# Residual sums of a graph-network stack: accumulating transfers in place of GpSimd sums, and a re-drawn order

## The chip, the cores and the metric

The kernel runs on one core of a Trainium2 chip. A core has five engines that run side by side, each through its own list of instructions in order: PE (TensorE, matrix products), DVE (VectorE), ACT (ScalarE), POOL (GpSimd) and SP (SyncE, which here only issues transfers). They wait for each other by semaphores. Transfers (DMA) run on 16 engines of their own. The metric is the time of one execution on the device in microseconds; the median of several runs counts, and less is better.

## What is computed

128 graphs of 64 nodes with 256 features go through four layers, each a residual step: normalise, rectify, apply a graph network, add to the input.

```python
# layers 0 and 1: attention over the neighbours
h = jnp.maximum(_layernorm(x, axis=-1), 0.0)
x = x + _L0_gnn_ref(h, adj, ...)     # 4 heads, ends in elu(...)
h = jnp.maximum(_layernorm(x, axis=-1), 0.0)
x = x + _L1_gnn_ref(h, adj, ...)     # 1 head, ends in elu(...)
# layer 2: products gated by a relation, summed over neighbours, relu
h = jnp.maximum(_layernorm(x, axis=-1), 0.0)
x = x + _L2_gnn_ref(h, nodemask, adj, ...)
# layer 3: three steps of a gated recurrence
h = jnp.maximum(_layernorm(x, axis=-1), 0.0)
x = x + _L3_gnn_ref(h, adj, ...)
# inside layer 3, three times:
#   m = h @ weight[i];  aggr = A^T m;  h = gru_cell(aggr, h)
```

Everything is float32. The change concerns the additions `x + ...` of layers 0, 1 and 3.

## The kernel before

**Tiling.** The 8192 rows of x are cut into 16 groups of 512 rows (8 graphs). A group's x lies in SBUF as the tile `xg`, 128 partitions by 4 by 256. For each group the layers 0, 1 and 2 run once (`first_layer`, `second_layer`, `third_layer`), then `before` normalises for layer 3, and a `Recurrence` object runs its three steps. Two groups' recurrences are interleaved with the first three layers of later groups, so that PE always has something of another group to do. Groups 0 and 1 are cut finer and take other ways through the early layers (`AHEAD = 2`); "from the third group on" means `g >= AHEAD`.

**Layers 0 and 1** are `attention(g, ...)`: statistics of `xg` on DVE (`st`, `mv`), `rstd` and `nm` on POOL, normalised values on ACT (`hn`), a transposition by DVE and through DRAM (`way`), products `mm` on PE, the attention factors `t` on DVE, and the weighted sums on PE into `o`. It ends in `elu_add` (line 850): with e = exp(min(o, 0)), the tile `em` becomes max(e - 1, o), and `engine.tensor_tensor(src, src, em, ALU.add)` adds it to `xg`. In the profile `em` is called hn, since it takes one of the three shared buffers of that name; the sum is the row xg<-xg,hn. The next layer's statistics read `xg` after it.

**Layer 3.** A step works out gates by products of 128x128 blocks with 256 columns (tiles `sy` and `sz`), each result picked up by DVE or ACT and put together in `hT`, `r` and `z`, partly by DVE instructions with two SBUF operands (`hT<-r,hT`, `r<-z,r`), partly by POOL (`r<-hT,hT`, and `aS`, `hS`, sums of the next step's operands). After the last step the state is brought back through DRAM (`back_by_dma`, into `hnat`), `finish` (line 1054) adds it to `xg` on POOL (row xg<-xg,hnat), and SP stores the result. The very last group instead turns its result on PE and adds on DVE.

**The order.** The program does not emit as it goes. A recording layer (`Plan`) notes every operation with an estimated cost, `forward` lists them engine by engine by due time, `backward` works out new due times, and `emit` (line 504) repeats this `PASSES` times from a random `SEED`, keeps the best, then shifts the due times of whole jobs by the pseudo-random moves named in `MOVES`, and emits the outcome once. All operations so recorded carry line 550 in the profile (blocks of 64x64 products line 842). So new numbers in `SEED` and `MOVES` mean another order on all engines. A transfer is planned with an issue time of `ISSUE` = 665 ns on its engine and a landing worked out from `cost` (line 584). Where the planner leaves PE idle in the first 115 us, `emit` puts warm-up products (line 1664) whose results nobody reads.

Of the kernel before, what the change touches and what calls it, by code (L numbers as in the profile page):

```python
# [13 lines left out]
ALU = mybir.AluOpType  # L14
# [3 lines left out]
S = 32  # L18
# [3 lines left out]
K = D // P  # L22
# [200 lines left out]
class Plan:  # L223
# [30 lines left out]
    def note(self, engine, call, cost, writes, reads, after=(), port=0.0, dma=False):  # L254
# [23 lines left out]
            b.ops.append(op)  # L278
        return op

    PASSES, SEED, SPREAD = 40, 35, 50.0
    MOVES = (
        10, 23, 28, 30, 40, 45, 69, 85, 99, 108, 114, 116, 126, 132, 141, 159, 210, 227, 236, 241, 319, 326, 339, 343,
        354, 365, 383, 426, 448, 489, 544, 596, 636, 646, 651, 652, 704, 736, 741, 742, 743, 752, 760, 807, 869, 944,
        951, 987, 991, 1089, 1101, 1110, 1124, 1248, 1251, 1273, 1452, 1492, 1498, 1501, 1678, 1834, 1893, 1966, 2005,
        2010, 2196, 2270, 2336, 2377, 2433, 2441, 2584, 2658, 2695, 2697, 2873, 3006, 3016, 3031, 3058, 3081, 3167,
        3224, 3271, 3376, 3444, 3459, 3524, 3571, 3664, 3704, 3719, 3750, 3772, 3786, 3953, 4165, 4169, 4192, 4344,
        4481, 4581, 4610, 4913, 4970, 5115, 5123, 5266, 5287, 5433, 5732, 6133, 6139, 6156, 6871, 6933, 7088, 7813,
        7842, 8883, 9045, 9231, 9268, 10172, 10189, 10284, 10634, 10814, 10991, 13029, 13068, 13352, 13896, 14140,
        16577, 16772, 17027, 533, 1980, 2724, 3643, 4767, 7708,  # L290
    )
    LEEWAY = {"PE": 100.0, "DVE": 100.0, "Activation": 100.0, "Pool": 100.0, "SP": 300.0, "-": 0.0}
    OVERLAP = {"DVE": 83.0, "Activation": 95.0, "Pool": 43.0}
# [35 lines left out]
    def forward(self):  # L329

        for b in self.bases:
            b.left, b.end, b.spot = len(b.ops), 0.0, None
        pools = {id(b.pool): b.pool for b in self.bases}.values()
        for pool in pools:
            pool.clear()
        for op in self.ops:
            op.job.left, op.waits = op.job.size, len(op.after)
        free = dict.fromkeys([*ENGINES.values(), "-"], 0.0)
        ready = {e: [] for e in free}
        held = {"DVE": 0.0, "Pool": 0.0}  # L340
        wire, parts = 2500.0, False
        order, self.replaced = [], []

        def enter(op):
            t = 0.0
            for other, data in op.after.items():
                late = other.end + self.LATENCY
                if other.engine == op.engine and not (other.dma and data):
                    late = other.start if op.engine in ("PE", "SP") or not data else other.end + 35.0
                if late > t:  # L350
                    t = late
            op.ready = t
            ready[op.engine].append(op)

        def spots(op, t):

            places = []
            for b in op.needs:
                if b.spot is None:
                    taken = [tag for x, tag in places if x.pool is b.pool]  # L360
                    tag = b.pool.place(b, taken)
                    if tag is None:
                        return None, t
                    places.append((b, tag))
                    t = max(t, b.pool.released(tag, b, taken.count(tag)))
            return places, t

        for op in self.ops:
            if not op.waits:
                enter(op)  # L370
        while len(order) < len(self.ops):
            best = None
            for e, ops in ready.items():
                leeway, first, found = self.LEEWAY[e], 1e18, []
                for op in ops:
                    t = op.ready if op.ready > free[e] else free[e]
                    if t > first + leeway or best is not None and t > best[0] + leeway:
                        continue
                    if any(j.left for j in op.job.after):
                        continue  # L380
                    places, t = spots(op, t)
                    if places is not None:
                        first = min(first, t)
                        found.append((t, op, places))
                found = [(t, op.due, op, places) for t, op, places in found if t <= first + leeway]
                if found:
                    found = min(found, key=lambda f: (f[1], f[0]))
                    if best is None or found[:2] < best[:2]:
                        best = found
            assert best is not None, "nothing can be emitted"  # L390
            t, _, op, op.places = best
            e = op.engine
            ready[e].remove(op)
            for b, tag in op.places:
                old = b.pool.put(b, tag)
                if old is not None:
                    self.replaced.append((old, op))
            if e == "-":
                for pool in pools:
                    pool.open = True  # L400
            op.start, op.idle = t, t - free[e]
            if op.dma:
                free[e] = t + self.ISSUE
                wire = max(wire, t + 1350.0) + op.cost
                op.end = wire + 400.0
            else:
                took = op.cost
                if e == "PE":
                    took -= self.TURN if op.parts and parts else 0.0
                    parts = op.parts  # L410
                elif op.port:
                    other = "Pool" if e == "DVE" else "DVE"
                    took = max(took, held[other] + min(op.port, took) - t)
                    held[e] = t + took
                op.end = t + took + (165.0 if e == "PE" else 0.0)
                free[e] = t + took - op.overlap
            for b in op.bases:
                b.left -= 1
                b.end = max(b.end, op.end)
            op.job.left -= 1  # L420
            order.append(op)
            for other in op.then:
                other.waits -= 1
                if not other.waits:
                    enter(other)
        return max(free.values()), order

    def backward(self, end):
# [12 lines left out]
        for op in self.ops:  # L441
            op.took = min(op.end - op.start, 4500.0) if op.dma else op.end - op.start
            op.held = (op.took if op.engine in ("DVE", "Pool") else op.cost) - op.overlap
            if op.dma:
                op.held = self.ISSUE
            op.rank = op.end + self.random.gauss(0.0, self.SPREAD)

        def limit(op, late):
# [135 lines left out]
def cost(engine, method, args, kwargs):  # L584

    n = elements(args[0])
    if engine == "tensor":
        m = elements(args[2] if method == "matmul" else args[0])
        return (m / 1.2 + 2.5) * (1 if method == "transpose" else 2)
    if engine == "sync" or method == "dma_start":  # L590
        to, of = args[:2]
        tag = to.base.tag if isinstance(to, View) else None
        rate = {"way": 450.0, "fine": 220.0, "t0": 190.0, "t1": 190.0}.get(tag, 150.0 if tag in (None, "at", "eg", "o", "row0", "row1") else 290.0)
        if isinstance(of, View) and of.base.tag in ("way", "fine"):
            rate = 170.0 if of.base.tag == "way" else 125.0
        return n * to.shape[0] * 4 / rate
    if engine == "vector":
        if method == "bn_stats":
            return 400.0
        if method == "tensor_reduce":  # L600
            n = elements(args[1])
        plain = method == "tensor_scalar" and not any(isinstance(a, View) for a in args[2:4])
        return 150.0 + n * (0.53 if plain and n >= 512 else 1.04)
    if engine == "scalar":
        return 150.0 + 0.86 * n if method in ("copy", "mul") else 310.0 + 0.73 * n
    if ALU.pow in args:
        return 1000.0
    return 200.0 + 2.1 * n if method != "memset" else 100.0 + 0.85 * n
# [3 lines left out]
def kernel(  # L612
# [237 lines left out]
    def elu_add(work, src, o, engine, by_scalar=False):  # L850
# [6 lines left out]
            nc.vector.tensor_scalar(em, o, 0.0, None, op0=ALU.min)  # L857
            nc.scalar.activation(em, em, AF.Exp)
        nc.vector.scalar_tensor_tensor(em, em, -1.0, o, op0=ALU.add, op1=ALU.max)
        engine.tensor_tensor(src, src, em, ALU.add)  # L860

    def block_diagonal(dst, src, scalar, op):

# [116 lines left out]
    class Recurrence:  # L980
# [72 lines left out]

        def finish(self):

            to = self.src.rearrange("p n (k i b) -> p (n k) i b", k=K, b=S)
            nc.gpsimd.tensor_tensor(to, to, spread(self.hnat), ALU.add)
            self.store(self.src, slice(None))

        def step(self, i, back=True, in_parts=False):  # L1060
# [159 lines left out]
    with ExitStack() as s1:  # L1220
# [175 lines left out]
        def attention(g, p0, n, layer, heads, we, pool):  # L1396
# [59 lines left out]
                edges = mt[:, q : q + m, None, :].to_broadcast([P, m, heads, N])  # L1456
                nc.vector.tensor_tensor(t4, t4, edges, ALU.min)
            o = aggregate_graphs(pool, psum, t, wv, heads, g < 16)
            elu_add(pool, src, o, nc.vector if g < 1 else nc.gpsimd, g >= AHEAD)

        def first_weights():
            e0 = once.tile([P, K, 2 * H], F32, name="e0")
# [419 lines left out]
```

## Time and profile before

| | us |
|---|---|
| runs | 1311.43, 1312.52, 1318.44; median 1312.52 |
| the profiled execution | 1311.0 |
| its span, first to last instruction | 1309.2 |
| first product of the recurrence starts at | 95.3 |
| last product of 256 columns starts at, on PE | about 1298 |

Busy shares of the span are 98% for PE, 80% for DVE, 66% for ACT and 53% for POOL; the granted PE clock is 0.997 of full speed. A row of the profile gives engine, operation, destination tile, source tiles, shapes, how often, the total and mean time, and the idle time of the engine just before such instructions with what ended it. "L550" is the line of the recording layer and says nothing about the place; one goes by the tiles. A product of 32-bit numbers appears as two MATMUL records, and the end of a record is modelled: starts are what one can trust.

The chain of work that ended last runs through PE for 86% of the span, through DVE for 6%, through POOL and ACT for 3% each. The views that the prediction is worked out from are shown there.

### The profile page before, as it was taken

To read this page: it belongs to the slowest core of one execution; us is meant where nothing else is said; L and a number is where in the kernel's file an instruction comes from. 1 tells how busy PE (TensorE), PEld (TensorE's weight loads), DVE (VectorE), ACT (ScalarE), POOL (GpSimd) and SP (SyncE) were. 2 spreads that over 40 slices of the span, in tenths; PEclk is the share of its full clock that TensorE was granted. 3 is DMA by queue.
4 is the path that set the end of the run, shared out by engine and by line. 5 is a ranking of instruction groups with operands and counts; after the bars stand their busy time and mean duration, and the time that the engine had idled before them with its cause. 6 is when DMAs were issued, how large, how long until landed. Compare 5 with 4: busy or idle time off the path is not lost.

```text
span 1309.2 us, 27708 instructions
## 1 busy us (share of the span) xinstructions
PE 1288.8 (98%) x9761; PEld 1024.4 (78%) x9761; DVE 1052.5 (80%) x2532; ACT 857.7 (66%) x2179; POOL 700.3 (53%) x859
## 2 busy tenths in 40 slices
PE   9999999999999999999999999999999999999996
PEld 8667877788777887777787787778878787778885
DVE  7887788968879798887968879796969877776665
ACT  7876666766667676666657657766766667655543
POOL 4845454645555473655527456373747556435443
PEclk9999999999999999999999999999999999999998
DMA  8202133343343434334333444433334433322112
GB/s 249 87 19 63 33 118 106 112 128 118 118 125 111 141 98 135 131 104 122 128 112 114 121 136 122 130 130 102 118 98 138 146 86 117 104 77 71 60 65 69
DMA packets 139349, 142.64 MB, mean 109 GB/s; under 512 B 46912, under 2 KB 126272, under 8 KB 139200
## 3 DMA queue, kind: packets, MB, share of 16 engines
q1 hardware_dynamic: 137856, 140.50, 35.1%
q8 instruction: 80, 1.31, 0.4%
q14 instruction: 69, 0.57, 0.1%
q10 hardware_dynamic: 1344, 0.27, 0.1%
HBM read 78.39 MB, written 61.80 MB: 107 GB/s over the span
## 4 chain that ended last, share of the span: by engine, by line
PE 86%; DVE 6%; POOL 3%; ACT 3%; issue 1%; DMA 1%; SPq 0%; DVEq 0%; ACTq 0%; POOLq 0%
PE sy L550 35%; PE sz L550 26%; PE mm L550 16%; PE mm L842 3%; PE tp L842 3%; DVE hT L550 2%; DVE t L550 1%; PE tp L550 1%; POOL rstd L550 1%; ACT hn L550 1%; PE sz L1664 1%; PE tq L842 1%; POOL xg L550 1%; DVE r L550 1%; DMA t<-row 1%
## 5 line engine op out<-in xcount | busy, mean ns | idle before, releaser
L550 POOL TENSOR_TENSOR r<-hT,hT 128x256 f32<-128x256 f32 x192 | 154.4, 811 | 237.7 <-ACT hT L550 236.9
L550 DVE SCALAR_TENSOR_TENSOR hT<-r,hT 128x256 f32<-128x256 f32 (+1 forms) x290 | 186.4, 647 | 27.1 <-ACT r L550 24.7
L550 PE MATMUL sy<-aS,wsum 128*128 128x256 f32 x576 | 172.8, 384 | 1.9 <-DVE hT L550 1.9
L550 PE MATMUL sy<-hS,wsum 128*128 128x256 f32 x576 | 171.2, 383 | 2.0 <-ACT z L550 1.5
L550 PE MATMUL sz<-hS,whh 128*128 128x256 f32 x576 | 171.4, 383 | 0.6 <-DVE z L550 0.5
L550 PE MATMUL sz<-aS,wc 128*128 128x256 f32 x576 | 164.9, 382 | 0.9 <-DVE hT L550 0.9
L550 DVE TENSOR_TENSOR hT<-hT,sz 128x256 f32<-128x256 f32 x288 | 117.7, 410 | 42.6 <-PE sz L550 38.9
L550 ACT ACTIVATE hT<-hT,bi 128x256 f32<-128x256 f32 x192 | 95.8, 504 | 51.8 <-DVE hT L550 51.3
L550 PEld LDWEIGHTS sy<-hS,wsum 128*128 128x128 f32 x576 | 107.1, 190 | 27.8 <-issue 5.9
L550 POOL TENSOR_TENSOR rstd<-var,mhalf 128x4 f32<-128x4 f32 (+1 forms) x70 | 76.7, 1095 | 97.2 <-ACT var L550 92.5
L550 PEld LDWEIGHTS sy<-aS,wsum 128*128 128x128 f32 x576 | 107.2, 190 | 25.1 <-issue 6.0
L550 PEld LDWEIGHTS sz<-aS,wc 128*128 128x128 f32 x576 | 108.2, 190 | 21.6 <-issue 5.8
L550 PEld LDWEIGHTS sz<-hS,whh 128*128 128x128 f32 x576 | 107.5, 190 | 21.9 <-issue 5.9
L550 ACT ACTIVATE hT<-sy,bh 128x256 f32<-128x256 f32 x192 | 90.0, 469 | 49.8 <-PE sy L550 48.6
L550 POOL TENSOR_TENSOR aS<-aT 128x256 f32<-128x256 f32 x96 | 79.0, 823 | 81.6 <-ACT aT L550 78.8
L550 PE MATMUL mm<-wl,hT 128*128 128x512 f32 x248 | 118.9, 595 | 1.3 <-DVE u L550 1.0
L550 ACT ACTIVATE hn<-xg,nm,rstd 128x256 f32<-128x256 f32 x200 | 109.4, 594 | 15.1 <-POOL nm L550 11.9
L550 ACT COPY z<-sy 128x256 f32<-128x256 f32 x192 | 70.2, 369 | 66.8 <-PE sy L550 65.2
L550 DVE TENSOR_TENSOR hT<-hT,sy 128x256 f32<-128x256 f32 x192 | 79.2, 412 | 37.5 <-PE sy L550 35.1
L550 DVE TENSOR_TENSOR z<-sz,z 128x256 f32<-128x256 f32 x192 | 79.6, 416 | 25.7 <-PE sz L550 23.4
L550 DVE BATCH_NORM_STATS2 st<-xg 128x6 f32<-128x256 f32 x256 | 95.6, 406 | 5.1 <-DMA xg<-in_x_dram 3.1
L550 POOL TENSOR_TENSOR hS<-hT 128x256 f32<-128x256 f32 x96 | 81.8, 852 | 24.5 <-DVE hT L550 15.2
(212 smaller groups left out, 3197.9 us busy)
## 6 DMA issues: line engine op xcount, KB each, us to landing
way<-tb SPq DMA_DIRECT2D x59, 512.0 KB, 2.7
hnat<-way SPq DMA_DIRECT2D x184, 128.0 KB, 3.0
way<-hn SPq DMA_DIRECT2D x42, 512.0 KB, 3.0
hn<-way SPq DMA_DIRECT2D x168, 128.0 KB, 2.9
xg<-in_x_dram SPq DMA_DIRECT2D x15, 512.0 KB, 4.3
out_dram<-xg SPq DMA_DIRECT2D x15, 512.0 KB, 3.0
t<-row SPq DMA_DIRECT2D x28, 256.0 KB, 4.0
hT<-way SPq DMA_DIRECT2D x52, 128.0 KB, 2.9
```

The source lines that it names most:

```text
L550: return do(*[real(a) for a in args], **{k: real(v) for k, v in kwargs.items()})
L842: nc.nc.tensor.matmul(*[real(x) for x in product], start=True, stop=True)
L1664: nc.spare = lambda: psum.spare and nc.nc.tensor.matmul(pause, warm, warm, start=True, stop=True)
```

## The change

Three things change.

- `elu_add` gets no engine (`None`) in layers 0 and 1 from the third group on. Then it issues a transfer from POOL's queue that reads `em` and adds it to `xg` in place (`accum_op`), 512 KB, 28 times in all. The planner gets a cost for it (line 591 on: bytes / 200 per ns, so 2.6 us on the wire), and an issue time of 1000 ns on POOL.
- `finish` adds in two pieces of two row blocks each; the store still follows both.
- `SEED` and `MOVES` are new, so the order of all instructions is.

```diff
-    PASSES, SEED, SPREAD = 40, 35, 50.0
+    PASSES, SEED, SPREAD = 40, 47, 50.0
     MOVES = (
-        10, 23, 28, 30, 40, 45, 69, 85, 99, 108, 114, 116, 126, 132, 141, 159, 210, 227, 236, 241, 319, 326, 339, 343,
...
+        27, 28, 39, 43, 47, 48, 58, 65, 69, 92, 99, 136, 172, 201, 203, 236, 247, 266, 267, 280, 285, 286, 311, 315,
...
     )
...
             if op.dma:
-                free[e] = t + self.ISSUE
+                free[e] = t + (1000.0 if e == "Pool" else self.ISSUE)
                 wire = max(wire, t + 1350.0) + op.cost
...
             if op.dma:
-                op.held = self.ISSUE
+                op.held = 1000.0 if op.engine == "Pool" else self.ISSUE
...
     if engine == "sync" or method == "dma_start":
         to, of = args[:2]
+        if "accum_op" in kwargs:
+            return n * to.shape[0] * 4 / 200.0
...
         nc.vector.scalar_tensor_tensor(em, em, -1.0, o, op0=ALU.add, op1=ALU.max)
-        engine.tensor_tensor(src, src, em, ALU.add)
+        if engine is None:
+            nc.gpsimd.dma_start(src, em, accum_op=ALU.add)
+        else:
+            engine.tensor_tensor(src, src, em, ALU.add)
...
         def finish(self):
 
-            to = self.src.rearrange("p n (k i b) -> p (n k) i b", k=K, b=S)
-            nc.gpsimd.tensor_tensor(to, to, spread(self.hnat), ALU.add)
+            m = G // 2
+            for p in range(0, G, m):
+                to = self.src[:, p : p + m].rearrange("p n (k i b) -> p (n k) i b", k=K, b=S)
+                nc.gpsimd.tensor_tensor(to, to, spread(self.hnat[:, :, p : p + m]), ALU.add)
             self.store(self.src, slice(None))
...
-            elu_add(pool, src, o, nc.vector if g < 1 else nc.gpsimd, g >= AHEAD)
+            elu_add(pool, src, o, nc.vector if g < 1 else nc.gpsimd if g < AHEAD else None, g >= AHEAD)
```

In the built programs the counts of instructions differ only where the diff says so, and in the warm-up products: 48 before, 61 after. Before any recurrence product starts, both programs put the same kinds and nearly the same numbers of other products on PE.

## The prediction

> **What bounds the kernel now.** First the busy table and the busy time by stage. Columns of the second view: stage, its length, then busy us of PE, weight loads, DVE, ACT, POOL, granted clock, DMA share, GB/s.
>
> ```profile
> PE 1288.8 (98%) x9761; PEld 1024.4 (78%) x9761; DVE 1052.5 (80%) x2532; ACT 857.7 (66%) x2179; POOL 700.3 (53%) x859
> ...
> 95.00:1280.00 1185.00, 1177.65 (x8977) 943.07 (x8970) 961.82 (x2262) 773.35 (x1920) 639.26 (x757) 1.00 0.36 109
> 1280.00:1310.00 30.00, 18.79 (x84) 14.76 (x82) 16.67 (x35) 8.72 (x20) 8.74 (x9) 0.85 0.24 74
> ```
>
> PE is the bound, and in the long middle stage (95 to 1280 us) it is idle for only 7.4 us of 1185. But a matmul's recorded time ends later than its successor starts, so short gaps are inside "busy". I therefore read starts in the timeline: a product with 256 columns is two records and takes 0.43 us from start to start when nothing delays it (385.39 to 385.83 around the first stall below). Measured against such undisturbed pitches, PE loses in the middle stage: 11 stalls of at least 0.165 us, 9.1 us together; 140 gaps of about 0.105 us, 14.7 us together; and 116 similar gaps (11.0 us) in front of blocks of 64x64 tiles, which come with the blocks. So an order of work can win back at most 9.1 + 14.7 = 23.8 us here, 1.8% of the time.
>
> Next, who makes the long stalls. The groups of POOL and DVE that bear on it (busy us, mean ns; idle before):
>
> ```profile
> L550 POOL TENSOR_TENSOR xg<-xg,hn 128x1024 f32<-128x1024 f32 x28 | 69.4, 2478 | 22.8 <-DVE hn L550 22.8
> L550 POOL TENSOR_TENSOR xg<-xg,hnat 128x1024 f32<-128x1024 f32 x15 | 36.5, 2436 | 20.3 <-DMA hnat<-way 20.2
> ...
> L550 DVE SCALAR_TENSOR_TENSOR hT<-r,hT 128x512 f32<-128x512 f32 x94 | 82.2, 879 | 0.9
> ```
>
> and the timeline of POOL, DVE and PE at three stalls (start, length):
>
> ```profile
> 383.75 2.80 POOL L550 TENSOR_TENSOR xg<-xg,hn 128x1024 f32<-128x1024 f32 x1
> ...
> 384.60 2.50 DVE L550 SCALAR_TENSOR_TENSOR hT<-r,hT 128x512 f32<-128x512 f32 x1
> ...
> 385.83 0.59 PE L550 MATMUL sz<-hS,whh 128*128 128x256 f32 x2
> 387.90 0.70 PE L550 MATMUL sy<-hS,wsum 128*128 128x256 f32 x2 [1.48 <-ACT z L550]
> ```
>
> ```profile
> 524.16 2.43 POOL L550 TENSOR_TENSOR xg<-xg,hnat 128x1024 f32<-128x1024 f32 x1 [2.33 <-DMA hnat<-way]
> ...
> 524.29 2.91 DVE L550 SCALAR_TENSOR_TENSOR hT<-r,hT 128x256 f32<-128x256 f32 x2
> ...
> 525.94 0.59 PE L550 MATMUL sy<-aT,wsum 128*128 128x256 f32 x2
> 528.19 0.70 PE L550 MATMUL sy<-aS,wsum 128*128 128x256 f32 x2 [1.66 <-DVE hT L550]
> ```
>
> ```profile
> 1290.30 2.35 POOL L550 TENSOR_TENSOR xg<-xg,hnat 128x1024 f32<-128x1024 f32 x1 [6.65 <-DMA hnat<-way]
> ...
> 1291.10 1.83 DVE L550 SCALAR_TENSOR_TENSOR hT<-r,hT 128x256 f32<-128x256 f32 x1
> ...
> 1293.32 0.48 PE L550 MATMUL sz<-aS,wc 128*128 128x256 f32 x1 [0.87 <-DVE hT L550]
> ```
>
> In each, a DVE instruction with two SBUF operands starts inside POOL's long sum and does not end until POOL's has: 2.50 us where the same form takes about 0.7 us. The gate chain of the recurrence stands still behind it, and PE runs out of operands. Note 0.70 instead of 0.59 at the restart: after each wait another 0.11 us goes, which is what the 140 short gaps are.
>
> **What the Trainium skill says.** "SBUF — State Buffer", section "Who interferes with whom": a VectorE instruction with two SBUF inputs contends with a GpSimd instruction that reads SBUF, and the later one blocks fully. The lines above agree (2.50 us, ended by POOL's end at 386.55). The same page, section "SBUF: two separate sides": a transfer issued from GpSimd needs GpSimd to write descriptors, which VectorE in a two-port mode holds up; the trace of before has no such transfer. "DMA: Bandwidth & Descriptors", section "Rules for kernel authors": an accumulating transfer reads its destination and writes it later, so readers must wait for its semaphore; here that is the next layer's statistics. Price, same page, "Anatomy of one DMA": 2.0 us + bytes / 436 GB/s, so 3.2 us for 512 KB as an estimate, and about 1 us to the first byte (section "Specifications"). SP's transfers of that size land in 3.0 and 4.3 us:
>
> ```profile
> way<-hn SPq DMA_DIRECT2D x42, 512.0 KB, 3.0
> ...
> xg<-in_x_dram SPq DMA_DIRECT2D x15, 512.0 KB, 4.3
> ```
>
> **The change, part by part.** Against the span of 1309.2 us:
>
> 1. *28 sums leave POOL.* 69.4 us of POOL work go; 28 issues come. What each issue costs POOL is not in the trace: between 0 and the old 2.48 us, and I take 1 us. Queued behind it on POOL in the new order are the recurrence's own operations (r, hS or aS in nearly all cases), so they wait less than before. The gain is in the lock. Over the trace, DVE instructions with two SBUF operands run 82.6 us longer than their undisturbed length; 15.9 us of it (16 collisions) lie under xg<-xg,hn. PE's stalls that follow from these sums: 1.64 (386.0), 1.17 (639.0, where DVE's transpose waited for the sum's end) and 0.41 us (1027, the buffer of the summand free too late) = 3.2 us. All gone: -3.2.
>
> 2. *The 15 last sums in halves.* Each half should take some 1.2 us (the rows with 512 columns have a mean of 1315 ns). In the new POOL order the halves mostly stand next to each other (11 of 15 with nothing between), so a DVE instruction that comes during the first may get in between them or not. Stalls from these sums: 1.82 (526.2), 0.91 (219.8), 1.03 (1292.1) = 3.8 us; bounds 0 and -3.8; I take half: -1.9. Of their 8.9 us of DVE lock time half would go, 4.4.
>
> 3. *Short gaps.* DVE's lock loss falls by (15.9 + 4.4) / 82.6 = 25%. If the short gaps fell alike: 14.7 x 0.25 = 3.6; but many come from ACT or from the order, so I take half: -1.8.
>
> 4. *Another order.* All engines' orders are re-dealt. Of the 23.8 us some 16 are left after 1 to 3. Before's own remaining stalls (1.38 at 600.0, where the mask product waited for t<-row; 0.68 at 1140, POOL's rstd) are accidents of an order; a new one has its own. I see one thing in the new order that leaves room: between a sum's summand and the next statistics, DVE has 9 instructions (median), 4.4 us of work by the starts of such rows, where there were 6 to 7 with 2.8 us. Bounds: -12 and +6. I take -4.
>
> 5. *The start.* The program puts warm-up products where its planner left PE idle before 115 us: 61 instead of 48. At 0.22 us each that is 2.9 us more planned idleness ahead of the first recurrence step (the other products ahead of it, each at its pitch, are the same: 74.5 against 75.6 us). Bounds 0 and +2.9; part of it will sit in gaps that PE had anyway. I take +2.
>
> 6. *The wait for the landing.* Today the statistics follow the sum's end by some 0.5 us (median of the 28). Then: 1 us of issue and about 4 us to land (between the 3.0 and 4.3 above, and it reads two operands), 5 us from the summand. The new order's 4.4 us of DVE work take 4.4 / 0.81 = 5.4 us at DVE's 81% load of the middle stage. So the landing is just hidden where the order has its median; in five of the 28 places DVE has under 2.7 us of work there, and there DVE waits some 2 us, as it waited before for POOL. What stalled DVE by about 1 us 16 times cost PE 3.2 us, so 5 x 2 us cost some 2, less what other idle time covers. Bounds 0 and +17 (rival C). I take +1. The summand's buffer (three of them, shared) is held some 2.5 us longer too; the same cover.
>
> Turns into and out of 64x64 blocks stay: 128 blocks against 130. The DMA engines get 28 x 0.5 MB more to write at a share of 0.36: nothing.
>
> Sum: -3.2 - 1.9 - 1.8 - 4 + 2 + 1 = -7.9, so a span of 1301.3 us. The profiled execution took 1311.0 us, 1.8 more than its span; the median of the runs is 1312.5, another 1.5 above. Forecast for the median: 1312.5 - 7.9 = 1304.6 us, -0.6%. A measurement here tells no change from up to about 0.5%, 6.6 us, so the forecast lies barely outside.
>
> **The rivals.**
>
> *B, a draw.* The lock stalls go, but the new order earns nothing and the start costs in full: -3.2 - 1.9 - 1.8 + 2.9 + 1.5 = -2.5, 1310.0 us. For it: 11 long stalls in 1185 us is already few. Against it: the short gaps are half of what can be won, and DVE is freed of a quarter of its lock time.
>
> *C, slower: the landing at the head of DVE's queue.* The statistics stand in DVE's queue; if the landing is late, everything behind them (gates of the recurrence) stands. If issue to landing takes 7.5 us, because accumulation runs at half rate or descriptors wait, DVE stalls 2 us at 28 places, 56 us; at the 0.3 that PE lost per us of DVE's long blocks (3.2 of 15.9 us, plus its short gaps) that is +17: -2.5 - 1.5 + 17 = +13, 1325.5 us. It decides from about 6.5 us on, where the cost passes the 4 us saved plus the 6.6. Against it: 3.0 to 4.3 us for like transfers, and DMA engines idle two thirds of the time.
>
> *D, the order bears much more:* items 1 and 2 in full (-7.0), short gaps and remaining stalls halved (-10), +2: 1297.5 us.
>
> **How the numbers follow.** Forecast 0.50 (own range 1299 to 1309: 0.42 of it faster, 0.08 within 0.5%); B 0.30 (0.03, 0.26, 0.01 slower); C 0.12 (0.02 within, 0.10 slower); D 0.08, faster. Together: faster 0.53, within 0.5% 0.36, slower 0.11. The range 1297 to 1316 leaves out C and half of D.
>
> **What would show it.** Items 1 and 2: no DVE instruction of 2 us or more beside POOL; mean of the 128x512 form of hT<-r,hT down from 879 towards 800 ns. 3 and 4: starts of products 0.43 us apart with fewer breaks; idle PE in 95 to 1280 below 4 us. 5: the first product of sy later than its 95.3 us. 6: waits of DVE's st for the transfer into xg in sum below 10 us, landing near 4 us. Wrong would be: such waits above 30 us, landing above 6 us, or a first recurrence step 5 us later.

## The result, and the profile after

The kernel after takes 1326.43 us (median of 6 runs, 1324.90 to 1330.28), the one before 1312.68 us (6 runs, 1311.43 to 1318.44): a ratio of 1.0107, 95% interval 1.0090 to 1.0125. It is slower by 14 us, where the forecast was 1304.6 us and the range ended at 1316. The profiled execution took 1330.28 us with a span of 1328.5; it is the longest of the six, 3.9 us over their median, so single sums from it are read with that in mind.

The busy table and the busy time by stage of the kernel after (columns as before: stage, length, busy us of PE, weight loads, DVE, ACT, POOL, clock, DMA share, GB/s):

```profile
PE 1303.0 (98%) x9787; PEld 1028.0 (77%) x9787; DVE 1041.2 (78%) x2532; ACT 856.9 (65%) x2179; POOL 650.3 (49%) x874
...
95.00:1280.00 1185.00, 1170.59 (x8815) 925.86 (x8814) 940.15 (x2237) 764.55 (x1904) 581.23 (x760) 1.00 0.42 120
```

POOL is busy for 50 us less than before and DVE for 11 us less, as intended. Yet PE's idle time in the middle stage doubled, from 7.4 to 14.4 us. Measured from start to start against undisturbed pitches, as in the prediction, PE lost there:

| 95 to 1280 us | before | after |
|---|---|---|
| stalls of at least 0.165 us | 11, 9.1 us | 43, 22.3 us |
| gaps of about 0.105 us | 140, 14.7 us | 172, 18.2 us |
| gaps in front of 64x64 blocks | 116, 11.0 us | 108, 10.2 us |

The first product of the recurrence starts at 99.2 us instead of 95.3. So the 19.3 us between the two spans are 13.2 of long stalls, 3.5 of short gaps and 3.9 of a later start, less about 1.3 in turns and at the end. Seven of the 43 stalls are no waits: they are records of four products that ran at half clock, shown below.

Now the parts that the change touched. First POOL's and DVE's groups (busy us, mean ns of one; idle before):

```profile
L549 POOL TENSOR_TENSOR xg<-xg,hnat 128x512 f32<-128x512 f32 x30 | 39.6, 1334 | 19.4 <-DMA hnat<-way 18.3 <-issue 1.1
L549 POOL DMA_DIRECT2D xg<-hn x28 | 25.7, 920 | 8.5 <-DVE hn L549 8.5
```

```profile
L550 DVE SCALAR_TENSOR_TENSOR r<-z,r 128x512 f32<-128x512 f32 x94 | 78.9, 845 | 12.0 <-POOL r L550 5.9 <-ACT z L550 5.8 <-ACT hT L550 0.2
...
L549 DVE SCALAR_TENSOR_TENSOR r<-z,r 128x512 f32<-128x512 f32 x94 | 82.0, 878 | 15.1 <-POOL r L549 9.8 <-ACT z L549 4.9
L549 DVE SCALAR_TENSOR_TENSOR hT<-r,hT 128x512 f32<-128x512 f32 x94 | 75.3, 807 | 0.9
```

(The first of the last three lines is from before.) An issue holds POOL for 0.92 us. The form of hT<-r,hT with 512 columns fell from 879 to 807 ns, as it was to do, but r<-z,r did not: 845 before, 878 now. Then the transfers (queue; packets, MB and share; and the median from issue to landing) and DVE's waits for them (us in total, times, longest):

```profile
q0 software_dynamic: 4032, 14.68, 5.8%
...
xg<-hn POOLq DMA_DIRECT2D x28, 512.0 KB, 4.6
```

```profile
DVE st L549 <- DMA xg<-hn: 5.7, 5, 1.9
...
DVE hn L549 <- DMA xg<-hn: 2.9, 1, 2.9
```

A transfer lands 4.6 us after its issue, and DVE's statistics (st) wait for one at five places only, 5.7 us in all. By the prediction's own marks the landing was fine. Two other marks failed: PE's idle time was to be below 4 us and is 14.4, and no DVE instruction was to take 2 us or more beside POOL, where gates of 2.3 to 3.2 us now stand within 4 us of an issue at four places. The last line is another wait: DVE's transpose into hn does not read the sum, it wants the *buffer* of the summand, which the transfer holds until it lands. It makes the longest stall of PE. The timeline of POOL, DVE and PE there:

```profile
409.66 0.91 POOL L549 DMA_DIRECT2D xg<-hn  x1
410.60 0.74 POOL L549 TENSOR_TENSOR aS<-aT 128x256 f32<-128x256 f32 x1
```

```profile
410.75 0.62 DVE L549 TENSOR_SCALAR top<-amax 128x4 f32<-128x4 f32 x1
414.26 1.25 DVE L549 STREAM_TRANSPOSE hn<-hn 128x1024 f32<-128x1024 f32 x1 [2.90 <-DMA xg<-hn]
415.44 1.25 DVE L549 TENSOR_TENSOR u<-mm,bl 128x512 f32<-128x512 f32 x2
```

```profile
414.08 0.59 PE L549 MATMUL sz<-aT,wc 128*128 128x256 f32 x2
416.85 1.22 PE L549 MATMUL sy<-hS,wsum 128*128 128x256 f32 x2 [2.17 <-ACT z L549]
417.87 1.06 PE L549 MATMUL sy<-aS,wsum 128*128 128x256 f32 x2
418.72 1.06 PE L549 MATMUL sy<-hT,whh 128*128 128x256 f32 x2
```

DVE stands for 2.90 us, from 411.36 until the landing; u, ACT's gates behind it and then PE follow, 2.3 us late against an undisturbed pitch. That is not all that PE loses there. The restart takes 1.22 us and not 0.70, and the next products start 0.85 us apart and not 0.43. The busy time by stage says why; its last three columns are clock, DMA share and GB/s:

```profile
416.70:420.20 3.50, 3.35 (x8) 2.72 (x9) 3.50 (x12) 1.44 (x6) 0.59 (x1) 0.51 0.47 171
```

For about 3.4 us after the stall PE is granted half its clock. Four products take 3.45 us in place of 1.73, so another 1.7 us go: one late buffer costs PE 4.0 us. Between 95 and 1280 us the clock of the kernel before never falls so. The stall alone does not decide it: in e3 below, the same stall of 2.3 us at the same place leaves the clock at 1.00.

The profile suggests a culprit, but 9 us of waits do not add up to 14 with an order that changed everywhere. Hence the experiments.

### The profile page after: what moved, and what is told of

Read it like the earlier page. It is cut to its first block, busy times and chain, and to the rows that moved or that the text cites. A ratio compares the mean times of both kernels' runs of the same rounds, so it can differ in the third digit from the quotient of the medians.

```text
span 1328.5 us, 27819 instructions
## 1 busy us (share of the span) xinstructions
PE 1303.0 (98%) x9787; PEld 1028.0 (77%) x9787; DVE 1041.2 (78%) x2532; ACT 856.9 (65%) x2179; POOL 650.3 (49%) x874
## 4 chain that ended last, share of the span: by engine, by line
PE 82%; DVE 6%; DMA 5%; ACT 2%; issue 2%; POOL 1%; SPq 1%; DVEq 0%; ACTq 0%; POOLq 0%
PE sy L549 33%; PE sz L549 24%; PE mm L549 16%; PE mm L843 3%; PE tp L843 3%; DMA xg<-hn 2%; DVE hT L549 2%; DVE r L549 1%; PE sz L1670 1%; PE tp L549 1%; DVE hn L549 1%; DMA t<-row 1%; ACT hn L549 1%; DMA row<-fT 1%; PE tq L843 1%
## 5 line engine op out<-in xcount | busy, mean ns | idle before, releaser
L549 POOL TENSOR_TENSOR r<-hT,hT 128x256 f32<-128x256 f32 x192 | 158.6, 838 | 258.4 <-ACT hT L549 257.9
L549 DVE SCALAR_TENSOR_TENSOR hT<-r,hT 128x256 f32<-128x256 f32 (+1 forms) x290 | 175.4, 611 | 34.5 <-ACT r L549 32.6
L549 PEld LDWEIGHTS sz<-aS,wc 128*128 128x128 f32 x576 | 107.6, 190 | 19.3 <-issue 2.9
L549 DVE SCALAR_TENSOR_TENSOR r<-z,r 128x512 f32<-128x512 f32 (+1 forms) x98 | 83.5, 859 | 15.1 <-POOL r L549 9.8
```

The costliest lines, as they stand in the source:

```text
L549: return do(*[real(a) for a in args], **{k: real(v) for k, v in kwargs.items()})
```

## The experiments

Most of them keep an order fixed. `note` records an operation for the planner with a cost and a set of reads and writes; what is emitted in its place can be another. With the recorded part unchanged, PE, DVE, ACT and SP keep their lists instruction for instruction, and only the operation in question differs (in e10, SP's list gains the 28 issues). Ratios are to the kernel before, timed beside each run; its medians there lay between 1312.93 and 1313.99 us. "The sums" are the 28 residual sums of layers 0 and 1 from the third group on.

### Order against mechanism

**e1: the new order, with sums on POOL.**

```diff
-            nc.gpsimd.dma_start(src, em, accum_op=ALU.add)
+            add = lambda: nc.nc.gpsimd.tensor_tensor(real(src), real(src), real(em), ALU.add)
+            nc.note("Pool", add, elements(src) * P * 4 / 200.0, [src], [em], dma=True)
```

> The changed kernel's order on every engine, instruction by instruction, but the 28 transfers are POOL sums again. Theory T (the transfers' landings cost the time): about 14 us come back, 1308 to 1314 us. Rival O (the new order costs the time, the transfers little or nothing): stays at 1322 us or above, since the long sums under the same order add POOL's lock again. A result between 1315 and 1321 splits the loss.

1347.21 us (1343.96 to 1348.91), 1.0249 (1.0230 to 1.0268).

**e2: the old order, with transfers.**

```diff
-        engine.tensor_tensor(src, src, em, ALU.add)
+        if nc.on and by_scalar:
+            add = lambda: nc.nc.gpsimd.dma_start(real(src), real(em), accum_op=ALU.add)
+            nc.note("Pool", add, 200.0 + 2.1 * elements(src), [src], [src, em], port=50.0 + 2.1 * elements(src))
+        else:
+            engine.tensor_tensor(src, src, em, ALU.add)
```

> The order of before on every engine, but the 28 POOL sums of the groups from the third on are accumulating transfers from POOL's queue. T: the statistics follow the sum too closely there, DVE waits some 2 to 3 us at most of the 28 places, 1325 to 1340 us. O: the lock stalls of these sums (3.2 us) go and the landings cost about as much, 1308 to 1316 us.

1371.47 us (1369.61 to 1376.05), 1.0438 (1.0420 to 1.0455). DVE's waits in it (us in total, times, longest):

```profile
DVE st L550 <- DMA xg<-hn: 53.5, 24, 4.7
...
DVE hn L550 <- DMA xg<-hn: 6.7, 2, 3.7
```

Put together: in the old order sums take 1312.7 and transfers 1371.5; in the new one sums take 1347.2 and transfers 1326.4. Each order fits only what it was planned for, so neither "the landing" nor "the order" alone explains the loss: theory O was right of e1 and far off in e2, theory T the reverse, and even T's number for e2 was too small. With the order fixed the new mechanism can't be judged from the old order, and the new order can't be judged with the old mechanism. What is needed is what each order costs with the sums gone.

### The last sums in halves

**e3: the kernel after, last sums whole. e4: the kernel before, last sums in halves.** Both orders are kept; in e4:

```diff
-            nc.gpsimd.tensor_tensor(to, to, spread(self.hnat), ALU.add)
+            of = spread(self.hnat)
+            nc.note("Pool", self.halves, 200.0 + 2.1 * elements(to), [to], [to, of], port=50.0 + 2.1 * elements(to))
...
+        def halves(self):
+            for p in range(0, G, 2):
+                to = real(self.src)[:, p : p + 2].rearrange("p n (k i b) -> p (n k) i b", k=K, b=S)
+                nc.nc.gpsimd.tensor_tensor(to, to, spread(real(self.hnat)[:, :, p : p + 2]), ALU.add)
```

and in e3 the reverse: nothing at the first half, the whole sum at the second.

> The changed kernel, same order, but the 15 last sums are whole again. Halves worth 1.9 us (the prediction's item 2): about 2 us slower than the changed kernel, 1328 us; up to 6 us slower if DVE got between the halves; within 1 us if it did not.

> The kernel before, same order, the 15 last sums in halves. Item 2 as predicted: 1310.5 us, 1.9 us faster; no gain if POOL's second half takes the port before the waiting DVE instruction: 1312.5 us.

e3: 1333.09 us (1332.13 to 1336.54), 1.0159 (1.0139 to 1.0178), so the halves are worth 6.7 us in the new order, more than the 6 that were expected at most; why was not looked into. e4: 1310.82 us (1309.33 to 1312.52), 0.9978 (0.9964 to 0.9993): worth 2 to 3 us in the old order. e4 beats both kernels, if by little.

### What the transfers cost in the new order

**e5: the transfer adds em to itself** (nobody reads what lands). **e6: nothing in its place. e7: the order before, with nothing in the place of the sums.**

```diff
-            nc.gpsimd.dma_start(src, em, accum_op=ALU.add)
+            add = lambda: nc.nc.gpsimd.dma_start(real(em), real(em), accum_op=ALU.add)    # e5
+            add = lambda: None                                                            # e6
+            nc.note("Pool", add, elements(src) * P * 4 / 200.0, [src], [em], dma=True)
```

> The order of the kernel after, instruction for instruction, and its 28 transfers from the third group on, but each adds em to itself in place instead of to the residual tile: nobody reads what lands, and only the buffer of em is released by it, as before. Left out of the computation: the 28 residual sums of layers 0 and 1 from the third group on. Theory W (the readers' waits for the landing are what is lost): the time falls by 10 us or more, to 1316 or less. Theory O (the new order is a dearer one, whatever lands when): within 5 us of 1326.4, so 1321 to 1328; the waits of DVE for a landing named in the profile, about 9 us in six places of which some 5 us reach PE, are then all that can go.

> The order of the kernel after with nothing in the place of its 28 transfers: neither issue (0.92 us of GpSimd each) nor landing. Left out of the computation: the same 28 residual sums. Theory W: the same time as with the landing unread, 1316 or less, since the issue holds only GpSimd. Theory O: 1318 to 1325. If the 26 us that GpSimd spends issuing are what delays its later sums, the time lies 4 us or more under that with the landing unread.

> The order of the kernel before with nothing in the place of the 28 GpSimd sums from the third group on (last sums whole). Left out of the computation: the same 28 residual sums. It measures what these sums cost in the order that was planned with them: my prediction has 3.2 us for the sums and 1.8 us for short gaps, so 1307.7; if the order had no slack of its own and the sums only fill idle time of GpSimd, 1312. Against the same omission in the new order it is also the difference of the two orders with this work gone: theory O wants the new order at least 10 us above it, theory W within 5 us.

e5: 1325.68 us (1322.94 to 1326.54), 1.0085 (1.0053 to 1.0116). e6: 1313.99 us (1311.66 to 1314.99), 0.9997 (0.9984 to 1.0010). e7: 1310.06 us (1305.72 to 1314.67), 0.9967 (0.9956 to 0.9978). With the landing unread nearly all the loss is still there: theory W falls. With nothing issued it is gone: theory O, whose number e5 had met, falls too, since the same order without transfers is no slower than the kernel before. 11.7 us hang on the issue and on what the transfer holds. e7 lies between its two expectations (1307.7 and 1312). The orders themselves, without the sums, differ by 3.9 us, the halves of the new one included.

**e9: the same issues, with half a KB moved. e10: the same bytes, issued from SP.**

```diff
+            one = lambda: real(em)[(slice(None),) + (slice(0, 1),) * (len(real(em).shape) - 1)]
+            add = lambda: nc.nc.gpsimd.dma_start(one(), one(), accum_op=ALU.add)    # e9
+            add = lambda: nc.nc.sync.dma_start(real(em), real(em))                  # e10
```

> The order of the kernel after with its 28 transfers cut to one element of each partition, em to itself: GpSimd issues a transfer at each of the 28 places, and half a KB moves instead of 512. Left out of the computation: the 28 residual sums of layers 0 and 1 from the third group on. Theory I (the issue on GpSimd is what costs: the sums queued behind it run back to back and hold a two-operand instruction of DVE until the last of them): 1322 to 1326, if the issue takes about 0.9 us here too. Theory M (the moving of 14.7 MB is what costs): 1314 to 1317, as with nothing issued.

> The order of the kernel after with its 28 transfers issued from SP, em to itself without the sum: the same bytes move at about the same time, and GpSimd issues nothing. Left out of the computation: the same 28 residual sums. Theory I: 1314 to 1318, the three microseconds over the order with nothing issued being the one wait for the buffer of em near 410 us. Theory M: 1322 to 1326. SP's queue now waits for em in order, so transfers behind it may start later; where the time is above 1326, that is the reason and the run tells nothing.

e9: 1319.39 us (1317.27 to 1320.74), 1.0041 (1.0025 to 1.0057). e10: 1313.46 us (1312.02 to 1315.45), 1.0006 (0.9996 to 1.0015). e9 lies between the two theories. Moving 14.7 MB more as plain copies costs nothing that the runs resolve (e10 against e6), and the issue on POOL alone costs 5.8 us (0.0044 of 1313): half of the 11.7 that theory I had put down to it. The rest, another 5.8 us, comes only when the issue is POOL's and the bytes are many. (e10 changes two things at once, the issuing engine and the kind of transfer: it copies and does not accumulate.) The landings in e9 and in e10 (median us from issue to landing):

```profile
hn<-hn POOLq DMA_DIRECT2D x28, 0.5 KB, 2.1
```

```profile
hn<-hn SPq DMA_DIRECT2D x28, 512.0 KB, 3.0
```

and POOL's issue in e9, which is as long with half a KB as with 512:

```profile
L863 POOL DMA_DIRECT2D hn<-hn x28 | 25.8, 921 | 9.9 <-DVE hn L549 9.9
```

How 0.92 us of an engine with half its time idle costs PE something is seen where the two runs part. Around the 17th transfer, POOL and then DVE without any issue (e6):

```profile
719.06 1.54 POOL L549 TENSOR_TENSOR r<-hT,hT 128x256 f32<-128x256 f32 x2 [2.27 <-ACT hT L549]
721.08 0.73 POOL L549 TENSOR_TENSOR r<-hT,hT 128x256 f32<-128x256 f32 x1 [0.48 <-ACT hT L549]
...
720.08 1.07 DVE L549 SCALAR_TENSOR_TENSOR r<-z,r 128x512 f32<-128x512 f32 x1
```

and with the small issue (e9), where PE too is shown:

```profile
722.28 0.92 POOL L863 DMA_DIRECT2D hn<-hn  x1
722.94 1.70 POOL L549 TENSOR_TENSOR r<-hT,hT 128x256 f32<-128x256 f32 x2
...
722.50 2.69 DVE L549 SCALAR_TENSOR_TENSOR r<-z,r 128x512 f32<-128x512 f32 x1
...
726.66 0.70 PE L549 MATMUL sy<-hS,wsum 128*128 128x256 f32 x2 [0.58 <-ACT r L549]
```

Without the issue POOL's third r comes 0.48 us after the second, and DVE's r<-z,r, whose operands both lie in SBUF, is through in 1.07 us. With it two of POOL's r have queued up behind the issue, run back to back, and DVE's instruction ends 0.55 us after the second of them (725.19 against 724.64): 2.69 us. The same happens near 490 us, where DVE's hT<-r,hT takes 3.46 us in e9 and 0.68 us in e6 (POOL and DVE in e9):

```profile
488.70 1.03 POOL L549 TENSOR_TENSOR aS<-aT,aS 128x256 f32<-128x256 f32 x1
489.39 1.02 POOL L549 TENSOR_TENSOR aS<-aT 128x256 f32<-128x256 f32 x1
490.07 1.01 POOL L549 TENSOR_TENSOR aS<-aT,aS 128x256 f32<-128x256 f32 x1
490.76 1.00 POOL L549 TENSOR_TENSOR hS<-hT 128x256 f32<-128x256 f32 x1
...
488.87 3.46 DVE L549 SCALAR_TENSOR_TENSOR hT<-r,hT 128x512 f32<-128x512 f32 x1
```

Four sums of POOL start 0.69 us apart, each before the record of the one ahead has ended, and DVE waits for all four. Sums without a pause between them are not enough for that: in e6, POOL runs five in a row there too (from 484.54 us on), 1.1 to 1.6 us apart, and DVE gets in between. What closes that gap behind an issue is not shown. The issue by itself does not hold DVE: of the 14 instructions hT<-r,hT and r<-z,r that start inside an issue in e9, seven take their own 0.67 to 0.68 us, two of them wholly inside it; the other seven take 1.6 to 3.5 us, with a sum of POOL close behind the issue. In the kernel after, six DVE instructions of over 1.75 us start within 4 us of an issue, in e9 seven; in e6 only one of that length is left in the whole span (near 1089 us, 2.22 us), which e9 has as well.

Matching the ACT instructions of e9 and e6 one to one, e9 falls behind by 0.9 us near 222, by 1.3 near 490 and by 1.3 near 723, each time at such a DVE instruction: 3.5 of the 5.4 us between the two spans. Another 1.0 us comes near 1189, with no issue for 39 us before it: POOL's rstd takes 2.49 us there in place of 1.28, beside gates of DVE that have the same timing in both. The rest lies behind the last product. So the 5.8 us between the runs are measured, and some 3.5 of them are traced to this mechanism.

At 20 of the 28 places POOL's next instruction follows the issue at once (within 0.2 us). At 14 of these it follows its predecessor as closely in e6, without any issue. So at half of the places the issue went into a queue that had no pause, which it delays. Whether it would be cheap where POOL is idle behind it is not shown.

The second half is the buffer. The transposes of DVE near 410 us, in e5 and then in e9:

```profile
413.44 1.25 DVE L549 STREAM_TRANSPOSE hn<-hn 128x1024 f32<-128x1024 f32 x1 [2.96 <-DMA hn<-hn]
```

```profile
410.48 1.25 DVE L549 STREAM_TRANSPOSE hn<-hn 128x1024 f32<-128x1024 f32 x1 [0.44 <-ACT hT L549]
```

Matched in the same way, e5 falls behind e9 by 4.1 us between 387 and 439 us, and by about 1.4 us in all the rest up to the last product. One wait of 2.96 us for the summand's buffer, held until the transfer has landed, carries most of the other 5.8 us: a stall of PE of 2.4 us, and then 3.4 us at half clock (from 415.9 us; e6, e9 and e10 have no such stretch between 95 and 1280 us), which cost 1.7. From SP the same bytes land 1.7 us earlier (3.0 against 4.7), and that wait is 1.1 us at the most.

Last, e5 against the kernel after: 1.0085 against 1.0107. Reading what lands costs some 2.9 us more by the ratios, 0.75 by the medians; the intervals overlap.

### How much room the landings have

**e11: the kernel after with each transfer moved back on POOL, behind the sums that queue up after it.**

```diff
+            if held and (op.start > held[0].start + 3000.0 or op.engine == "Pool" and idle >= 900.0):
+                held.pop().call()
...
-            op.call()
+            if op.engine == "Pool" and op.dma:
+                held.append(op)
+            else:
+                op.call()
```

> The kernel after with each of the 28 transfers moved back in GpSimd's order to just ahead of the next GpSimd instruction before which the plan has 0.9 us of idle time, at most 3 us later; all else in the same order, and nothing left out. Theory I: the sums no longer wait behind the issue, so 5 to 10 us go of the 11.7 us between the landing unread and nothing issued, less what the later landings cost: 1316 to 1322. If the delay of the sums is not what costs: 1326 to 1332, from the later landings.

1373.89 us (1373.06 to 1375.80), 1.0462 (1.0438 to 1.0487): far above both expectations.

```profile
DVE st L554 <- DMA xg<-hn: 55.4, 22, 5.8
```

It gives no verdict on theory I, because the repair brought a larger cost of its own: 22 of the 28 landings now come too late. The new order had made just the room that a landing needs and no more. In the kernel after DVE waited for five, in the old order (e2) for 24.

**e12: the order before, with transfers that nobody reads.**

```diff
-            add = lambda: nc.nc.gpsimd.dma_start(real(src), real(em), accum_op=ALU.add)    # e2
+            add = lambda: nc.nc.gpsimd.dma_start(real(em), real(em), accum_op=ALU.add)     # e12
```

> The order of the kernel before with the 28 GpSimd sums of layers 0 and 1 from the third group on replaced by transfers of em to itself. Left out of the computation: these 28 residual sums. Against 1371.5 with the real transfers it splits the 58.8 us that the transfers cost in that order into issue and landing: theory W for this order (the landing comes too late for an order that reads the sum 2 us after it) has 1312 to 1320; if the wait is for the buffer of em, not for the residual tile, the time stays over 1340.

1333.68 us (1332.01 to 1340.51), 1.0165 (1.0126 to 1.0204), between the two expectations. Of e2's excess 37.8 us by the medians (35.8 by the ratios) come with the reading of what lands; 23.6 us (26.0), against e7, are the issue and the held buffer, twice what they cost in the new order. Both parts hold some half clock: e2's trace has six such stretches between 95 and 1280 us, 23.8 us together, and e12's two, 10.2 us. So the new order did earn something: it took the readers' part from some 37 to about 1 to 3 us and the issue's part from some 25 to 11.7.

### What an order is worth

**e8: the kernel after without its list of shifts. e13: the kernel before without its list.**

```diff
-    MOVES = ( ...
+    MOVES = ()
```

> The kernel after with the planner's list of shifts emptied: the same operations and costs, ordered by the planner's passes alone. It measures how much an order can be worth with all instructions the same. If the list of the kernel after is a good one for the chip, the time rises by 10 us or more (1336 or more); if it is no better than any other order, it stays between 1316 and 1336.

> The kernel before with the planner's list of shifts emptied: the counterpart of the same edit on the kernel after, which left its time at 1326.6. Theory S (the old list was worth much on the chip and the new one is worth nothing, which is why the new order's floor is no lower): 1320 or more. Theory P (lists of shifts are worth nothing on the chip in either kernel, and the loss is the transfers' alone): 1309 to 1316.

**e14: the kernel after with `SEED` and `MOVES` of the kernel before. e15: the kernel before with the halves known to the planner,** with its own `SEED` and `MOVES`:

```diff
-            to = self.src.rearrange("p n (k i b) -> p (n k) i b", k=K, b=S)
-            nc.gpsimd.tensor_tensor(to, to, spread(self.hnat), ALU.add)
+            m = G // 2
+            for p in range(0, G, m):
+                to = self.src[:, p : p + m].rearrange("p n (k i b) -> p (n k) i b", k=K, b=S)
+                nc.gpsimd.tensor_tensor(to, to, spread(self.hnat[:, :, p : p + m]), ALU.add)
```

> The kernel after with the seed and the list of shifts of the kernel before: same operations and planned costs, a third order for them. If the issue, the held buffer and the landing cost 12 to 15 us in any order that is planned for transfers, the time is 1320 to 1336; an order that escapes them shows as 1316 or less.

> The kernel before with the last sums in halves and nothing else of the change, the halves known to the planner, with the seed and shifts of before: the order is dealt anew, where the earlier run with halves kept the old order and took 1310.8. Theory S: a new order loses what the old list had found, 1316 to 1328. Theory P: 1308 to 1314.

| | us | ratio (95% interval) |
|---|---|---|
| e13, sums, no shifts | 1324.31 (1323.67 to 1325.98) | 1.0089 (1.0063 to 1.0115) |
| e8, transfers, no shifts | 1326.57 (1325.41 to 1328.72) | 1.0093 (1.0063 to 1.0122) |
| e14, transfers, old shifts | 1330.65 (1328.26 to 1333.22) | 1.0140 (1.0109 to 1.0170) |
| e15, sums, halves planned, old shifts | 1336.09 (1332.41 to 1337.87) | 1.0168 (1.0137 to 1.0199) |

The old list of shifts is worth 10.7 us on the chip (8 to 15 by the interval), together with the operations that it was made for. Given others to order it gains nothing: the transfers take 1330.65 with it and 1326.57 without any list, and halving 15 sums, which gains 2 to 3 us in the old order, loses 22 us when the plan is dealt anew (e15, above even theory S; the halves were not planned without a list). The code says why it does not carry over: `move` picks the jobs that it shifts by their planned mean start, so the same numbers shift other jobs once the plan differs. The new list is worth nothing that the runs resolve: 1326.57 without it, 1326.43 with it. Between the two plans without lists the sums and the transfers stand 2.3 us apart, inside their intervals. Part of the old list's worth is at the start: the first product of the recurrence comes at 95.3 us in the kernel before, at 99.0 in both plans without lists, and at 99.2 in the kernel after.

## Why the prediction was wrong

Three terms of its sum failed: the issues on POOL, put at nothing (5.8 us measured), the summand's buffer, put at nothing (5.8), and the new order, which was to gain 4 us and lost time. The sum by its own steps, in us, from ratios times 1313:

| step | predicted | shown by | measured |
|---|---|---|---|
| 1 and 3, the sums leave POOL | -5.0 | e7 | -4.3 |
| 2, halves | -1.9 | e4 | -2.9 |
| 4 and 5, the new order and its start | -2.0 | e6 against e7, less step 2 | +6.8 |
| 1, the issues | 0 | e9 against e6 | +5.8 |
| 6, the summand's buffer, half clock included | 0 ("the same cover") | e5 against e9 | +5.8 |
| 6, the readers of the landing | +1 | after against e5 | +2.9 |
| sum | -7.9 | | +14.1 |

The rows are taken in this sequence and add up by it. With the halves at their worth in the new order (6.7 us, e3), the row of the order would be +10.6. The readers' row is 0.75 by the medians. The 14 us can also be split another way: 10.7 for the old list that was given up (e13), 2.3 (0.5 by the ratios) for transfers and halves in place of sums with no list on either side, and nothing for the new list. The table says where the time goes within the new order, this split what the change cost against a plan that nobody had tuned.

- **Step 1** was right about the sums and wrong about what replaces them. It gave an issue 1 us of POOL (0.92 measured) and then charged nothing, because POOL's own operations "wait less than before". It compared the issue with the sum that goes, and not with nothing. Against nothing, an issue delays what stands behind it on POOL, with no pause at 20 of 28 places, and at three places the sums so delayed caught one of DVE's two-operand instructions, for 3.5 us in all (e9 against e6). The prediction had read the lock correctly on before's long sums, and did not ask where a new one would form. The Trainium skill ("SBUF — State Buffer", section "Who interferes with whom") says that whoever issues first blocks the other for the whole instruction; e9's 3.46 us show that a blocked DVE instruction can stand through a whole run of short ones, 0.68 us being its own length.
- **Step 2** has the right sign and is too small: 2.9 against 1.9 in the old order, 6.7 in the new one.
- **Step 3**, the short gaps, is not borne out by the profile. With the sums simply gone (e7) there are 138 such gaps and 14.5 us, against 140 and 14.7. The 4.3 us that left with the sums cannot be split between stalls and gaps from one execution.
- **Step 4** has the wrong sign. It saw room in the order for the landing and took that for room in general: -4, with bounds of -12 and +6. The measured +6.8 includes step 5's +2; the first product starts 2.3 us later in e6 than in e7, 3.9 us later in the profile of after than in that of before. What it did not weigh is in its own words that remaining stalls "are accidents of an order; a new one has its own". The old order had few because it was a chosen one: e13 shows its list to be worth 10.7 us, and nothing in the profile of before said that a new list would be worth as much. Four new deals of the work (e8, e13, e14, e15) stand at 1324 to 1336 us, with sums or with transfers; the kernel after lies among them.
- **Step 6** got the landing right (some 5 us from the summand; 4.6 measured from issue, DVE's st waiting 5.7 us of the 10 it allowed) and disposed of the buffer in half a sentence. Held for 4.6 us instead of 2.5, it was late once, for 2.9 us, at a place with nothing behind it to hide it. PE stalled for 2.3 us and then had half its clock for 3.4 us, which took 1.7 more; the prediction has no term for that. This place explains 4.1 of the 5.8 us. No run gave the summand another buffer, so the row rests on e5 against e9 and on the traces of this place.

Rival C gave 1325.5 us, almost the time measured, by a mechanism that did not happen: a landing of 7.5 us and 28 stalls of the statistics. Its place, the head of DVE's queue, was right for one instruction, and the reason was a buffer. That its number fits is luck. Of the 22 us between forecast and fact, the issue's cost at zero makes 5.8, the order's gain 8.8 and the buffer 5.8.

Left open: whether transfers with a list of shifts searched for them on the chip would beat the kernel before. With the sums gone altogether the new order stood at 1314.0 us and the old at 1310.1, so the room that any replacement of these sums had is about 3 to 4 us in the old order. Also not tried: a fourth buffer for the summand, which would itself change the plan.

## What to carry to other kernels

Cost what replaces a removed operation against nothing, not against what it replaces: list what stands behind the new instruction on its engine, and ask which shared resource the pile will hold. Do not count a stall of the main engine by its length alone: here 2.3 us of waiting brought half clock for 3.4 us more. A transfer frees the engine but holds its source buffer until it lands, so the next writer of that buffer is a reader of the landing, too. In a tuned order any edit that lets the planner deal anew has to earn back what the old order was worth; measure that first by emptying its list, and try the edit with the order kept (e4) before planning it (e15): here the same edit was worth -2 to -3 us one way and +22 the other.

## What the runs showed of the hardware

- An issue from GpSimd takes 0.92 us, for 512 KB (kernel after) as for 0.5 KB (e9).
- The same 512 KB inside SBUF lands 4.7 us after an issue from GpSimd with accumulation (e5) and 3.0 us after a plain one from SP (e10); half a KB from GpSimd lands after 2.1 us (e9); all are medians. Whether accumulation or the queue makes the difference was not separated.
- 14.7 MB of extra plain copies, issued from SP beside the recurrence, cost no time that the runs resolve (1313.46 us in e10, 1313.99 in e6), with the DMA engines some two fifths busy (0.39).
- A DVE instruction with two SBUF operands can stand behind several short GpSimd instructions in a row: 3.46 us in place of 0.68, behind four that start 0.69 us apart (e9).
- A GpSimd issue does not hold such a DVE instruction by itself: two ran wholly inside an issue in their own 0.68 us (e9).
- A stall of PE of 2.3 to 2.4 us was followed by some 3.4 us at half clock, with products 0.85 us apart and not 0.43 (kernel after, e5); the same stall in e3 was not.
